# A gated state-space layer and a mixture of experts on one core: the front and first loop of the scan reordered, half a convolution given to TensorE, a new last tile, and new interleaving tables

## The chip, the cores and the metric

The kernel runs on one core of one Trainium2 chip. A core has five engines that run side by side, each with its own in-order instruction queue: TensorE (PE, matmuls; its weight loads are shown as PEld), VectorE (DVE), ScalarE (ACT), GpSimd (POOL) and SyncE (SP, which issues most DMAs). The metric is the time on the device of one execution, in microseconds (us). Three timed runs of the kernel before gave 1078.26, 1078.32 and 1080.39 us, a median of 1078.32 us. A further execution was recorded by the hardware profiler; every duration in this document that is not called a median comes from such a profiled execution.

## The reference

Four independent sequences `b`, each of L = 512 tokens. A state-space layer runs over a context and is gated by the normalised input; its result is added to the input, and a mixture of seven experts (three per token, beside one shared expert) is added to that.

```python
x   = einsum('ed,bld->bel', in_proj_w, ctx)               # 512 channels, from 256
u   = silu(causal_conv(x, conv_w, 4 taps) + conv_b)       # one filter per channel
dt, Bm, Cm = split(einsum('ke,bel->bkl', x_proj_w, u))    # 16, 16, 16 rows
delta = softplus(dt_proj_w @ dt + dt_proj_b)
for t:                                                    # scan over time, n = 16 states
    state = state * exp(delta_t * A) + (delta_t * u_t) * B_t
    y_t   = sum_n state * C_t
y = (y + D * u) * silu(layernorm(x_in))
x = x_in + tanh(g0) * y
x = x + tanh(g1) * moe(layernorm(x))                      # silu(x W1) * (x Wg) @ W2, top 3 of 7, plus shared
```

All arithmetic is fp32.

## The kernel before

**Layers and loops.** Sequence `b` is called layer `b`. Its 512 channels lie in four blocks `c` of 128 partitions, its 512 tokens in the free dimension. The scan of a layer (`loop`, from L495) goes in 32 steps; a step is one state `k` (of 16) and two channel blocks `c0`, `c0 + 1` (W = 2). For each step:

- POOL multiplies B by delta times u into `h` (`product`, L583, 1024 elements a partition);
- ACT makes the decay exp(delta A) into two PSUM banks `da` (`decay`, L594), of which there are only two in all;
- DVE runs two scans over time in `h` (L616), then multiplies `h` by C (`finish`, L541). The multiplication is called the C product here.

In layer 0 PE adds the C products of all states up in four PSUM banks `sum` by multiplying with the identity (L555), and every third C product is made by POOL rather than DVE. The C row is read from SBUF (`bc`) in the first four steps; from the fifth on ACT has copied it to a PSUM bank `c_bank` (L543) first. In layers 1 to 3 DVE makes all C products and adds them up itself (L548).

**What precedes a loop.** `in_proj` (PE, L246) fills a PSUM bank `pin`; `last_tap` (ACT, L256) and `other_taps` (DVE, L266, three instructions) are the convolution; `silu` (ACT, L272); `x_proj` (L278), `rows_out` and `load_bc` send B and C out to DRAM and back to all partitions; `dt_proj` (L298), `abs_relu`, `exp`, `log`, `rest_of_z`, `soft` make delta, `mul` (L358) the product u delta, and `d_u` (ACT, L351) the term D u. For layer 0 `front` (L425 on) does this with nothing beside it, and begins layer 1's convolution. The rest of layer 1's convolution stands in layer 0's first step (L628), all four `silu`s of layer 1 and the four gates `silus_x` are flushed after the second step (L633), and layer 1's delta is made a piece at a time during the loop (`ahead_delta`, called from `finish`, L530).

**Experts.** When a loop is done, `post` (L676) and `route` (L755) make the normalised rows and the routing, and `experts` (L990 on) the shared expert and 13 tiles of 128 routed rows, each with three weights loaded from DRAM. A tile takes 24 passes of 512 columns through PE, 8 of 128 for transposes, and a few instructions on ACT and DVE; its rows are added to the output by an indirect DMA that POOL issues (`add_rows`, L962). While the experts of sequence `q` run, the loop of layer `q + 1` and the preparation of layer `q + 2` run beside them. Their order is not left to a scheduler. `experts` is a generator with some 54 slots, and after each slot the table `STEPS[q]` says how many steps of the scan to emit and `PIECES[q]` how many pieces of the next layer's preparation. The tables thus fix in which order each in-order engine meets the work of the two. For the last sequence there is no loop left, and PE works alone.

**DMA queues.** SP issues the B and C loads (two buffers `bc`, each holding two states), the weights and the clearing of the sorted rows in DRAM (`clear`), all in program order; a load that waits for its buffer holds up what is behind it.

Where the wait lists below say `issue`, no other engine is seen to be waited for.

## Time and profile before

| what | us |
|---|---|
| median of the three timed runs | 1078.32 |
| the profiled execution | 1076.32 |
| its span, first to last instruction | 1074.5 |
| DVE busy in the span | 798.7 (74%) |
| PE busy | 948.9 (88%) |
| ACT busy / POOL busy | 544.5 / 493.7 |
| first scan of layer 0 starts | 39.80 |
| fourth C product of layer 0 done, fifth step's scans start | 69.19 |
| first transposes after loop 0 / 1 / 2 / 3 (L689) | 166.72 / 398.84 / 621.47 / 840.36 |
| mean granted TensorE clock | 0.953 |

A line of the timeline reads: start, duration, engine, source line, operation, output<-input, shape, count and, in square brackets, how long the engine had been idle before and what released it. Adjacent instructions of one kind are merged ("x4" is four of them, with one start and the busy time of all). The groups of busy time count a matmul until its modelled end, so PE at 20.00 of 20 us is not PE at its peak. Only stretches in which the engine that sets the pace is idle, or does what could be done elsewhere, can be won.

### The profile page before, as it was taken

How to read it: one execution, taken by the hardware profiler on the slowest of the kernel's cores; microseconds unless marked ns; L12 is line 12 of the kernel's file. 1: busy time of each engine (PE TensorE's matmuls, PEld its weight loads, DVE VectorE, ACT ScalarE, POOL GpSimd, SP SyncE). 2: the span in 40 equal slices, each digit the busy share in tenths (PEclk: the TensorE clock that was granted, in tenths of full speed). 3: DMA queues.
4: the chain of work that ended last, by engine and by line, in shares of the span. 5: the costliest groups of instructions: out<-in, count | busy, mean ns of one | idle time of the engine just before them, and what ended most of it. 6: DMA issues, size and time to landing. Idle time of an engine off the chain costs nothing. (4 is left out here: it accounts for less than half of the span.)

```text
span 1074.5 us, 8875 instructions
## 1 busy us (share of the span) xinstructions
PE 948.9 (88%) x2504; PEld 425.3 (40%) x2504; DVE 798.7 (74%) x992; ACT 544.5 (51%) x761; POOL 493.7 (46%) x326
## 2 busy tenths in 40 slices
PE   7377766799999987999998988889999999999995
PEld 3122223344444433444344443334444534444442
DVE  5888987999999998899999999999986521100000
ACT  5567552356687854447696755536665220122121
POOL 1278981383563653563555545755554205011111
PEclk9679888899999999999999999989999999999998
DMA  4139730198999865589899936779999459999973
GB/s 135 51 130 320 272 117 1 39 339 293 349 324 352 309 233 188 173 321 362 296 335 307 356 110 208 280 245 371 367 375 317 142 163 314 336 321 323 333 242 82
DMA packets 138044, 272.11 MB, mean 253 GB/s; under 512 B 17135, under 2 KB 17135, under 8 KB 137983
## 3 DMA queue, kind: packets, MB, share of 16 engines
q1 hardware_dynamic: 126174, 244.19, 64.4%
q0 software_dynamic: 11328, 26.42, 10.7%
q10 hardware_dynamic: 480, 0.79, 0.2%
q8 instruction: 26, 0.43, 0.2%
q14 instruction: 36, 0.29, 0.1%
HBM read 230.65 MB, written 40.71 MB: 253 GB/s over the span
## 5 line engine op out<-in xcount | busy, mean ns | idle before, releaser
L583 POOL TENSOR_TENSOR h<-bc,home 128x1024 f32<-128x1024 f32 x128 | 309.7, 2426 | 254.1 <-DVE home L548 207.7
L923 PE MATMUL p<-w,turned_x 128*128 128x512 f32 x832 | 380.0, 601 | 16.1 <-ACT turned_x L915 5.4
L616 DVE TENSOR_TENSOR_SCAN h<-da,h 128x512 f32<-128x512 f32 x256 | 297.3, 1205 | 11.9 <-POOL h L583 7.6
L594 ACT ACTIVATE da<-home,a_neg 128x512 f32<-128x512 f32 x256 | 174.7, 689 | 228.7 <-DVE h L616 224.5
L923 PEld LDWEIGHTS p<-w,turned_x 128*128 128x128 f32 x832 | 154.6, 192 | 196.8 <-issue 169.6
L923 PE MATMUL po<-w,turned_h 128*128 128x512 f32 x416 | 189.7, 599 | 6.3 <-ACT yo L957 3.6
L962 POOL DMA_INDIRECT out_dram<-yo,row x52 | 92.8, 1785 | 190.2 <-ACT yo L957 156.8
L1097 DVE TENSOR_TENSOR h<-h,p 128x512 f32<-128x512 f32 x52 | 35.1, 674 | 144.6 <-PE p L923 138.0
L541 DVE TENSOR_TENSOR h<-h,bc 128x1024 f32<-128x1024 f32 x96 | 130.9, 1363 | 1.0
L548 DVE TENSOR_TENSOR home<-home,h 128x1024 f32<-128x1024 f32 x96 | 119.5, 1245 | 3.1
L555 PE MATMUL sum<-hc,ident 128*128 128x512 f32 x128 | 75.6, 743 | 39.7 <-DVE hc L541 22.5
L923 PEld LDWEIGHTS po<-w,turned_h 128*128 128x128 f32 x416 | 75.7, 192 | 84.6 <-issue 76.0
L875 POOL DMA_INDIRECT xs<-xn,place x48 | 55.5, 1157 | 47.7 <-issue 39.4
L915 ACT COPY turned_x<-pt_x 128x512 f32<-128x512 f32 x52 | 30.2, 580 | 74.2 <-PE pt_x L910 74.2
L594 ACT ACT_TABLE_LOAD x51 | 65.4, 1283 | 0.9
L957 ACT ACTIVATE yo<-po,weight 128x512 f32<-128x512 f32 x52 | 35.6, 684 | 54.7 <-PE po L923 49.2
L555 PEld LDWEIGHTS sum<-hc,ident 128*128 128x128 f32 x128 | 28.1, 231 | 85.7 <-DVE hc L541 30.6
L923 PE MATMUL p2s<-home,w_s 128*128 128x512 f32 x128 | 61.5, 626 | 0.0
L923 PE MATMUL p1s<-home,w_s 128*128 128x512 f32 x128 | 59.5, 603 | 1.7 <-ACT sgs L1017 1.7
L1056 PE MATMUL pos<-w_s,home 128*128 128x512 f32 x128 | 57.1, 596 | 4.3 <-DVE home L1020 2.3
L915 ACT COPY turned_h<-pt_h 128x512 f32<-128x512 f32 x52 | 30.1, 578 | 48.9 <-PE pt_h L910 48.9
L1158 ACT ACT_TABLE_LOAD x36 | 46.2, 1283 | 0.5
(141 smaller groups left out, 812.7 us busy)
## 6 DMA issues: line engine op xcount, KB each, us to landing
w<-in_w_dram SPq DMA_DIRECT2D x104, 1024.0 KB, 6.6
w<-in_wg_dram SPq DMA_DIRECT2D x52, 1024.0 KB, 11.2
bc<-rows SPq DMA_DIRECT2D x32, 1024.0 KB, 7.8
xt<-xs SPq DMA_DIRECT2D x52, 256.0 KB, 4.4
xs<-empty SPq DMA_DIRECT2D x12, 780.0 KB, 16.7
w_s<-in_ws_dram SPq DMA_DIRECT2D x8, 1024.0 KB, 10.0
xx<-in_x_dram SPq DMA_DIRECT2D x4, 1024.0 KB, 7.4
w_s<-in_wsg_dram SPq DMA_DIRECT2D x4, 1024.0 KB
```

The costliest lines, as they stand in the source:

```text
L541: engine.tensor_tensor(hc, h, c_k.unsqueeze(1).to_broadcast([P, W, L]), ALU.mult)
L548: nc.vector.tensor_tensor(y[:, c0 : c0 + W, :], y[:, c0 : c0 + W, :], h, ALU.add)
L555: nc.tensor.matmul(sums[c1 + w], ident, hc1[:, w, :], start=False, stop=(k1 == NS - 1))
L583: nc.gpsimd.tensor_tensor(h, b_k.unsqueeze(1).to_broadcast([P, W, L]), layer.u[:, c0 : c0 + W, :], ALU.mult)
L594: nc.scalar.activation(da, layer.delta[:, c, :], AF.Exp, scale=a_neg[:, c, k : k + 1])
L616: nc.vector.tensor_tensor_scan(h[:, w, :], da, h[:, w, :], 0.0, ALU.mult, ALU.add)
L875: put = nc.gpsimd.indirect_dma_start(xs[q % 2], bass.IndirectOffsetOnAxis(ap=place[:, t, k : k + 1], axis=0), xns[:, t, :], None)
L915: nc.scalar.copy(t, pt)
L923: nc.tensor.matmul(p[:, 0:n], lhs(c), rhs(c), start=(c == 0), stop=(c == NC - 1))
L962: nc.gpsimd.indirect_dma_start(acc, bass.IndirectOffsetOnAxis(ap=slot_of[q][1][:, i : i + 1], axis=0), yo, None, compute_op=ALU.add,)
L1056: nc.tensor.matmul(pos[t], hTs[:, c, ts(t, P)], ws.t[2][:, c, :], start=(c == 0), stop=(c == NC - 1))
L1158: nc.scalar.activation(hs[i], p1.pop(i), AF.Silu)
```

## The change

Lines with `-` are the kernel before. The parts are:

- **Front.** Six small matmuls on the identity ahead of everything (`WARM`). `d_u` for blocks 0 and 1 of layer 0 is issued before the last `silu`, for 2 and 3 right after the logarithms. The logarithms get tiles of their own, since `y` now holds D u. The statistics of x (`norm_x`) for three blocks stand ahead of the `z` instructions, and `rest_of_z` for three blocks ahead of the first `soft`. The taps of layer 1's block 1 stand after `mul(1)`.
- **Convolution by TensorE.** For blocks 2 and 3 of layer 1 POOL builds diagonal matrices of the four taps; ACT copies `pin` to SBUF (`copy_in`), PE applies the taps by shifted matmuls (`all_taps`) in pieces of `ahead_delta`, and ACT adds the bias (`taps_out`). Eight matmul calls more on PE, beside the six of WARM, and six tap instructions fewer on DVE.
- **First loop.** All steps run over blocks first and states second; the C row goes to `c_bank` before step one, so no C product of DVE reads `bc`; the silus of layer 1 (blocks 0 and 1) and the four gates are flushed right after the first decay; those of blocks 2 and 3 come in `ahead_delta`, in a group of their own.
- **Tail.** In the last tile of the last sequence, the outputs of the tiles before it are finished first, and the second product, gate, transposes and copies go in two halves of 256 columns (`in_halves`).
- **Tables.** New `STEPS` for sequences 0, 1 and 2 and new `PIECES` for 0 and 1. Their sums are the same (34, 34 and 29 steps, 43 and 43 pieces).

```diff
 STEPS = {
-    0: ("000000", "101011010100110100110111110111110101001101101201101001"),
-    1: ("100000", "201001010010101100110201210101110110001101201101100101"),
-    2: ("000001", "111011010010110100210101101100101111002000011101000000"),
+    0: ("000000", "101011010100110100110120111101110200010101111101101001"),
+    1: ("100000", "201001001010110100110201201101110100101101201101100101"),
+    2: ("000001", "201011010000110100110200011100200110101110200111000000"),
 ...
 PIECES = {
-    0: "000000000020212021101111112021011011102021200121200201",
-    1: "000000000201110211111021211200111200221022101001202001",
+    0: "000000002010112021101100222002011020220222010002201110",
+    1: "000000101100111111111012112002022101122210211002100001",
 ...
+    spin = ps_o.tile([P, L], F32, tag="po", name="spin")
+    for _ in range(WARM):
+        nc.tensor.matmul(spin[:, 0:P], ident, ident, start=True, stop=True)
 ...
+    for c in BY_TENSOR:                       # (2, 3)
+        taps[c] = two.tile([P, DCONV, P], F32, bufs=3, name=f"taps_{c}", tag="turned")
+        nc.gpsimd.tensor_tensor(taps[c], ident..., pr[:, c, CW : CW + DCONV]..., ALU.mult)
 ...
+        def copy_in(self, c):
+            nc.scalar.copy(self.u[:, c, :], self.pin.pop(c))
+        def all_taps(self, c, ks):
+            if ks[0] == 0:
+                self.pcv = spare(f"pcv_{self.b}_{c}")
+            for k in ks:
+                nc.tensor.matmul(self.pcv[:, k:], taps[c][:, DCONV - 1 - k, :], self.u[:, c, 0 : L - k],
+                    start=(k == 0), stop=(k == DCONV - 1))
+        def taps_out(self, c):
+            nc.scalar.activation(self.u[:, c, :], self.pcv, AF.Identity, bias=pr[:, c, CB : CB + 1])
 ...
     def ahead_delta(ly):
+        for c in BY_TENSOR:
+            ly.all_taps(c, (0, 1)); yield
+            ly.all_taps(c, (2, 3)); yield
+            ly.taps_out(c); yield
+        for c in BY_TENSOR:
+            ly.silu(c)
+        yield
         ly.x_proj()
 ...
     def front():
 ...
+        for c in range(W):
+            l0.d_u(c)
         l0.silu(NC - 1)
-        for c in range(2):
-            l1.conv(c)
+        l1.conv(0)
+        l1.last_tap(1)
 ...
+        for c in range(NC - 1):
+            norm_x(0, c)
         for c in range(NC):
             l0.abs_relu(c, by_vector=True)
 ...
-            l0.log(c, own=False)
-        for c in range(W):
-            norm_x(0, c)
-            l0.w_of_z(c)
+            l0.log(c, own=("sg", "yo")[c % 2])
         for c in range(W, NC):
-            norm_x(0, c)
+            l0.d_u(c)
+        norm_x(0, NC - 1)
+        for c in range(NC - 1):
+            l0.rest_of_z(c)
         for c in range(W):
             l0.soft(c)
             l0.mul(c)
-        l1.conv(2)
+        l1.other_taps(1)
+        l1.copy_in(2)
 ...                                            # loop
-            steps[per_load:] = [(k, c0) for k in range(NG, NS) for c0 in range(0, NC, W)]
+            steps = [(k, c0) for k in range(NS) for c0 in range(0, NC, W)]
 ...
-            if sums is not None and n >= per_load:
-                if n % 3 == 2 and n < last:
+            if sums is not None:
+                if n % 3 == 2 and per_load <= n < last:
                     engine, late = nc.gpsimd, True
                 else:
                     c_k = c_bank
 ...
+            if b == 0 and n == 0:              # right after the first decay
+                szs = silus_x(b)
+                for c in range(NC):
+                    if c not in BY_TENSOR:
+                        later.append(lambda c=c: nxt.silu(c))
+                flush()
 ...
             if b == 0 and n == 0:
-                nxt.conv(NC - 1)
-                for c in range(NC):
-                    later.append(lambda c=c: nxt.silu(c))
-                szs = silus_x(b)
-            if b == 0 and n == 1:
-                flush()
+                nxt.copy_in(NC - 1)
 ...                                            # experts, the last tile of all
-            if ends:
-                second_product(i)
+            if ends:
+                out(i - 2)
+                add_rows(q, i - 3, yos.pop(i - 3))
+                add_rows(q, i - 2, yos.pop(i - 2))
+                output(i - 1, (ps_h, "p1"))
 ...
         if ends:
-            output(i - 1, (ps_h, "p1"), lambda: turn_h(i))
+            out(i - 1)
+            add_rows(q, i - 1, yos.pop(i - 1))
+            in_halves(i)
+            out(i)
```

## The prediction

> **What bounds the kernel now.** I read the busy tenths in 40 slices first, then the timeline of the first 110 us on all engines, then each stage's list of waits, and last the timelines around the longest of them.
>
> The page's busy rows (each digit is a slice of 26.9 us):
>
> ```profile
> PE   7377766799999987999998988889999999999995
> DVE  5888987999999998899999999999986521100000
> ```
>
> Three regimes. In the first 6 slices (to 160 us) no experts can run: DVE sets the pace and PE is half idle. From slice 9 to 29 both are near full. From slice 33 PE is alone. Loop 0 is a pure prologue: routing needs all of it, so what is cut there moves everything behind it.
>
> The timeline from 0 to 110 us:
>
> ```profile
> 8.26 0.78 ACT L256 ACTIVATE home<-pin,pr 128x512 f32<-128x512 f32 x1 [0.97 <-PE pin L246]
> ...
> 37.30 2.32 DVE L266 SCALAR_TENSOR_TENSOR home<-pin,pr,home 128x511 f32<-128x511 f32 x3
> 39.80 2.34 DVE L616 TENSOR_TENSOR_SCAN h<-da,h 128x512 f32<-128x512 f32 x2 [0.18 <-POOL h L583]
> 43.59 2.32 DVE L266 SCALAR_TENSOR_TENSOR home<-pin,pr,home 128x511 f32<-128x511 f32 x3 [1.46 <-ACT home L256]
> ...
> 57.19 1.28 ACT L272 ACT_TABLE_LOAD   x1
> 58.49 2.19 ACT L272 ACTIVATE home<-home 128x512 f32<-128x512 f32 x4
> 59.99 3.33 DVE L541 TENSOR_TENSOR hc<-h,bc 128x1024 f32<-128x1024 f32 x1
> 60.59 2.92 ACT L487 ACTIVATE sz<-xx,nmr,rstd_z 128x512 f32<-128x512 f32 x4
> 65.61 2.34 DVE L616 TENSOR_TENSOR_SCAN h<-da,h 128x512 f32<-128x512 f32 x2 [2.29 <-POOL h L583]
> 69.19 2.33 DVE L616 TENSOR_TENSOR_SCAN h<-da,h 128x512 f32<-128x512 f32 x2
> ```
>
> To be seen: two tap groups of layer 1 on DVE between 37 and 46 us; two DVE waits (1.46, 2.29); a C product of 3.33 us where its like takes 1.22; and ACT busy for 7.6 us with silus and table loads just when DVE needs decays.
>
> Later waits, from the timelines of their places:
>
> ```profile
> 98.76 1.22 DVE L541 TENSOR_TENSOR hc<-h,c_bank 128x1024 f32<-128x1024 f32 x1 [2.59 <-ACT c_bank L543]
> 235.06 0.75 DVE L1062 SCALAR_TENSOR_TENSOR xx<-pos,tg,xx 128x512 f32<-128x512 f32 x1 [2.04 <-PE pos L1056]
> 460.58 0.69 DVE L1020 TENSOR_TENSOR home<-sgs,p2s 128x512 f32<-128x512 f32 x1 [2.09 <-ACT sgs L1017]
> 710.41 0.69 ACT L594 ACTIVATE da<-home,a_neg 128x512 f32<-128x512 f32 x1 [0.42 <-DVE h L616]
> 711.04 0.58 ACT L915 COPY turned_x<-pt_x 128x512 f32<-128x512 f32 x1
> 711.67 6.72 PE L923 MATMUL p<-w,turned_x 128*128 128x512 f32 x8 [3.08 <-ACT turned_x L915]
> 718.66 3.60 PE L923 MATMUL p<-w,turned_x 128*128 128x512 f32 x8
> 1058.92 1.54 POOL L962 DMA_INDIRECT out_dram<-yo,row  x1 [5.76 <-ACT yo L957]
> 1064.47 1.54 POOL L962 DMA_INDIRECT out_dram<-yo,row  x1 [4.01 <-DMA out_dram<-yo,row]
> ```
>
> **The change part by part.** All against the profiled execution, 1076.32 us.
>
> *WARM.* The first input matmuls start at 4.72 when their data land, and follow each other by 0.85 us; from 8.06 on by 0.43. ACT's first tap waits 0.97 for the fourth. At 0.43 each the fourth would end near 6.6, and ACT would be held by `a_neg` (7.05 to 7.29) instead. The six calls are 12 passes of a quarter length, 2.6 us at the slow pace, from about 1.5 us (the identity is ready at 1.4), so they end before 4.72. Bounds: 0 (PE is still slow) and -0.97. I take -0.6. TensorE: Matmul & The Clock Gate (Part 1, "What's actually happening") of the Trainium skill says that PE runs at half rate until it has been busy for a window of about 3.4 us, and that the window runs freely. By that rule 2.6 us and a pause of 0.7 may or may not be enough, and this term would be 0 or -0.97.
>
> *Front to the fourth C product, on DVE.* In both kernels DVE ends layer 1's block 0 at 22.3 (WARM aside). From there the new order on DVE is: three pairs of statistics at 0.83 (to 24.8), four `z` at 0.62 (27.3), the fourth pair and `ve` (28.35), three times `w` and `rest_of_z` at 0.45 + 0.73 (31.9). The first logarithm ends at 31.4 as before (ACT's relus, table loads and exponentials end up where they were; z is only 0.3 later and the exp table load at 25.66 covers it). Then two times `soft` and `mul` at 2.17 (36.25), the taps of block 1 at 2.3 (38.6), `nmr` 0.1, `soft` and `mul` of block 2 (40.8), block 3 with its `w` and rest 3.34 as at 50.78 (44.15). Four steps of scans and C product follow at 3.6, as the steps from 69.19 on: 58.55. Before: 69.19. This term is -10.6. It consists of two tap groups of 2.3 gone, 1.46 + 2.29 of waits, 2.1 of the long C product, and 2.5 of small gaps and of work moved into the wait for the logarithm.
>
> What must cover it: the two `d_u` ahead of the last `silu` are 1.44 of ACT in an idle time of 1.59 before 18.73. The taps' diagonals are two POOL multiplications (some 1.2 each by half of L583's 2.4), after `pr` lands near 7; POOL's next need is 28. ACT after the logarithms (33.0): two `d_u` 1.44, `copy_in` 0.57, C copy 0.57 (B and C have landed by 31.2, when DMA traffic ends), table load 1.28, two decays 1.3 (38.2), table load, four gates 2.92, two silus 1.1, table load: 44.8. The next decays need a bank that the first scan frees at 45.4, so ACT is on time by 0.6, under 5.5 us of DVE work on blocks 2 and 3; that is what the 7.6 us at 57.19 lacked. In layer 1's `in_proj(3)` PE now waits for block 1's taps, since both use the bank `s`; PE's next work is at 44, it has 5 us to spare. SP's third B and C load waits for its buffer until 52 instead of 69, so the shared weights and clears behind it start earlier.
> Bounds: -8 (the gates are 2.6 late) and -12.5.
>
> SBUF — State Buffer (Terms, "shared port pair") of the Trainium skill says that DVE and GpSimd lock a port pair for a whole instruction and the loser blocks. The row agrees once (3.33 is 1.22 plus most of one 2.35 POOL product) and not always (1.22 at 56.49 with POOL busy). By the rule the new order could also lose: `soft` and `mul` of blocks 2 and 3 read two SBUF tiles, and should the first POOL product (36.3 to 38.7) slip behind the taps they would block for up to 2.3, making this term -8.3.
>
> *Rest of loop 0.* The wait of 2.59 at 98.76 comes of ACT waiting 1.80 for a `pdt` that PE holds behind sums of late POOL products, after POOL had waited 2.09 for a B load. In the new order `dt_proj` is a step ahead of its reader and the load queue starts earlier, so I count it gone: -2.6. New is the second silu group: load 1.28, two silus 1.2, load 1.28 = 3.8 on ACT between decays. It begins 3.1 after a step's first scan starts, its next decay comes at 7.6, and DVE, whose step has its C product on POOL, wants it at 5.9: +1.7. Taps on PE (16 passes, 7 us) lie in PE's idle half; the two `taps_out` at 0.7 in ACT's gaps of 1.3 to 1.8 between decays. Sum -0.9; bounds -2.6 (burst hidden) and +3.8 (burst bare, the wait replaced by another: POOL has 9.23 of work in 9.4 per three steps).
>
> *Tail.* The last add is issued at 1064.47, after waiting 4.01 for the add before it, issued at 1058.92. Tile 11's output now goes ahead of tile 12's second product: its eight passes end at 1053.9, its add follows that of tile 10 (1051.61 + 4.8) at 56.9 and lands at 61.7. Tile 12: second product to 1057.4, gate half to 57.9, transposes 58.25, copy, output 3.44 to 61.9, scale 0.7: add at 62.9. -1.5. Bounds: -1.6, and +1 if short passes cost 0.25 rather than 0.215 each and the exposed gate counts twice.
>
> *Tables.* The instruction order of the two built programs shows what moves. Sequence 0: the taps of `pin_0` now stand ahead of the `pos` addition at 235.06, and fill its 2.04; DVE paces that stage: -2.0. Sequence 1: the same taps go ahead of the product at 460.58, filling 2.09: -2.1. Sequence 2: `turned_x_0` now precedes the decays at 709.30 and 710.41 that held it; PE would start 2.5 earlier and not fall to half pace (6.72 against 3.60 for eight): up to -5.6; DVE, full until 780, must follow, and I take -3.0. Together -7.1. I can't trace all other swaps of 43 + 43 pieces. Bounds: -13 (5.6, the POOL wait of 2.63 at 455.57, and others) and +6.2 (one new stall like that at 711).
>
> Sum: -0.6 - 10.6 - 0.9 - 1.5 - 7.1 = -20.7, so 1055.6 in a profiled execution. The median of the timed runs before stands 2.0 above the profiled one; carried over: **1057.6**.
>
> **The rivals.**
> - *The tables bring nothing*: their waits are replaced by others of the same size. For it: DVE and PE are both full there, and a moved instruction delays its neighbours. Against: the three waits are visibly uncovered. 1064.7.
> - *Loop 0 gives back*: POOL, full to 98%, becomes its bound, and the silu burst is bare. +4.7 on the forecast: 1062.3, and with idle tables 1069.4. For it: B loads kept POOL waiting three times (4.8 in all). Against: the loads come earlier now.
> - *More*: sequence 2 wins its whole 5.6 and the POOL wait of 2.63 goes: 1052.4, near 1050 with the bounds of the front.
> - *Slower*: the new tables put a PE input copy behind a pair of decays, as at 711, each time 6.2 (3.1 wait, 3.1 slow PE). Without the tables' gain the forecast is 1064.7; three such places make 1083.3, and above 13.6 / 6.2 = 2.2 of them it is slower than before. For it: the orders change in hundreds of places. Against: I find the copy moved ahead where it hurt.
> - *The warm-up doesn't warm*, or the halves save nothing: +0.6 to +2.1, inside the others.
>
> **How the numbers follow.** Forecast 0.48 (its own range 1052 to 1062), idle tables 0.25, loop 0 gives back 0.12, more 0.09, slower 0.05, and 0.01 for about no change. Low 1050 takes in most of "more"; high 1069 the idle tables and most of the give-back. Within 0.2% (2.2 us) is what a measurement here can't tell from no change. Faster 0.94, same 0.01, slower 0.05.
>
> **What would show it.** Right: the scans of layer 0 start near 44 without break; the fifth step's near 57 to 58; no DVE C product over 1.3 in loop 0; the first transposes at 153 to 156; the last add waiting for ACT, not a DMA; no idle DVE at the `pos` addition and no PE wait of 3 at sequence 2's first tile. Wrong: first scans past 47 with ACT as releaser; POOL as DVE's releaser in loop 0; stages between the first transposes longer than 232, 223 and 219.

## The result and the profile after

The changed kernel took 1059.36 us, the median of four executions (1056.93 to 1061.98); the kernel before, on the same chip, 1078.29 (four, 1075.84 to 1080.39). The ratio is 0.9825 with a 95% interval of 0.9802 to 0.9848: 18.9 us faster, where 20.7 were forecast. Six later executions gave a median of 1056.11 and, against the kernel before on the same chip, a ratio of 0.9812 (0.9784 to 0.9840). The profiled execution after took 1059.25 (span 1057.2), the one before 1076.32 (1074.5): 17.1 less.

The busy rows of the page after (a digit is now 26.4 us):

```profile
PE   9587867799999897999999888899999999999995
DVE  6999978999999997899999999888999531100000
```

The shape is the old one; the prologue is half a slice shorter, and DVE is at 6 or more in each of the first 30 slices. The timeline of the front and of loop 0 shows where that half slice went:

```profile
7.29 0.76 ACT L273 ACTIVATE home<-pin,pr 128x512 f32<-128x512 f32 x1
38.92 2.93 ACT L541 ACTIVATE sz<-xx,nmr,rstd_z 128x512 f32<-128x512 f32 x4
41.75 1.13 ACT L305 ACTIVATE home<-home 128x512 f32<-128x512 f32 x2
43.48 2.33 DVE L679 TENSOR_TENSOR_SCAN h<-da,h 128x512 f32<-128x512 f32 x2
45.85 1.22 DVE L595 TENSOR_TENSOR hc<-h,c_bank 128x1024 f32<-128x1024 f32 x1
56.48 1.22 DVE L595 TENSOR_TENSOR hc<-h,c_bank 128x1024 f32<-128x1024 f32 x1
57.62 2.33 DVE L679 TENSOR_TENSOR_SCAN h<-da,h 128x512 f32<-128x512 f32 x2
84.06 2.34 DVE L679 TENSOR_TENSOR_SCAN h<-da,h 128x512 f32<-128x512 f32 x2 [1.69 <-ACT da L648]
```

ACT's first tap (L273, formerly L256) no longer waits. Gates and silus now end at 42.9, ahead of the first scans at 43.48 (L679, formerly L616), and no wait stands between these and the fifth step at 57.62, which was at 69.19. All C products (L595, formerly L541) last 1.22. The wait of 2.59 for `c_bank` is gone; the one new wait in the loop is 1.69 at 84.06, for decays that stand behind the second group of silus.

The places that the tables were to improve, on DVE, with the POOL products beside two of them:

```profile
224.22 0.75 DVE L1120 SCALAR_TENSOR_TENSOR xx<-pos,tg,xx 128x512 f32<-128x512 f32 x1 [0.65 <-PE pos L1114]
224.88 1.82 DVE L595 TENSOR_TENSOR h<-h,bc 128x1024 f32<-128x1024 f32 x1
441.31 2.95 POOL L637 TENSOR_TENSOR h<-bc,home 128x1024 f32<-128x1024 f32 x1
441.46 0.69 DVE L1078 TENSOR_TENSOR home<-sgs,p2s 128x512 f32<-128x512 f32 x1 [2.09 <-ACT sgs L1075]
442.06 3.29 DVE L595 TENSOR_TENSOR h<-h,bc 128x1024 f32<-128x1024 f32 x1
452.13 3.99 DVE L595 TENSOR_TENSOR h<-h,bc 128x1024 f32<-128x1024 f32 x1
452.67 2.36 POOL L637 TENSOR_TENSOR h<-bc,home 128x1024 f32<-128x1024 f32 x1
```

The wait at the `pos` addition fell from 2.04 to 0.65, but the C product behind it now takes 1.82 instead of 1.21. In sequence 1 DVE's 2.09 for `sgs` is still there, at another instruction, and two C products run into POOL's (L637, formerly L583) and take 3.29 and 3.99.

To see what each part brought I cut both profiles at instructions that both kernels have. Layers are counted from 0; "old" columns are of kernels with the old code or table for that stretch, "new" of kernels with the changed one, over all profiles of this study.

| stretch | profiled pair, before / after | predicted change | old, mean (profiles) | new, mean (profiles) |
|---|---|---|---|---|
| start to layer 0's fifth step | 69.19 / 57.62 | -11.2 | | |
| from there to the first gate of layer 0 | 91.69 / 91.33 | -0.9 | | |
| start to that gate | 160.88 / 148.95 | -12.1 | 162.1 (2) | 147.4 (8) |
| gate to layer 1's first scan | 25.97 / 26.17 | 0 | | |
| layer 1's first scan to layer 2's (sequence 0) | 214.54 / 214.26 | -2.0 | 214.9 (4) | 214.0 (10) |
| layer 2's to layer 3's (sequence 1) | 223.23 / 223.67 | -2.1 | 224.1 (4) | 221.8 (10) |
| layer 3's to its router passes (sequence 2) | 244.49 / 239.01 | -3.0 | 243.9 (4) | 240.1 (9) |
| router passes to the last `pos` addition | 46.02 / 46.02 | 0 | | |
| `pos` addition to the last add to the output | 149.34 / 148.88 | -1.5 | 150.2 (2) | 148.9 (9) |
| last add to the end | 10.05 / 10.22 | 0 | | |

In the profiled pair the gain of 17.3 in the span is 11.9 up to the first gate, 5.5 in sequence 2, 0.5 in the tail, and nothing in sequences 0 and 1. The last two columns say that a single pair can mislead by 2 to 3 us in a stretch.

### The profile page after: what moved, and what is told of

The parts are those of the page before. It is cut to its first block, busy times and chain, and to the rows that moved or that the text cites. A ratio compares the mean times of both kernels' runs of the same rounds, so it can differ in the third digit from the quotient of the medians.

```text
span 1057.2 us, 8951 instructions
## 1 busy us (share of the span) xinstructions
PE 952.6 (90%) x2540; PEld 430.9 (41%) x2540; DVE 798.7 (76%) x987; ACT 551.5 (52%) x770; POOL 497.4 (47%) x328
## 5 line engine op out<-in xcount | busy, mean ns | idle before, releaser
L637 POOL TENSOR_TENSOR h<-bc,home 128x1024 f32<-128x1024 f32 x128 | 309.2, 2422 | 238.6 <-DVE home L602 200.0
L981 PE MATMUL p<-w,turned_x 128*128 128x512 f32 x824 | 374.5, 598 | 12.4 <-ACT h L1238 4.7
L679 DVE TENSOR_TENSOR_SCAN h<-da,h 128x512 f32<-128x512 f32 x256 | 297.5, 1206 | 9.3 <-ACT da L648 6.8
L981 PE MATMUL po<-w,turned_h 128*128 128x512 f32 x408 | 185.4, 598 | 7.7 <-ACT yo L1015 5.1
L1020 POOL DMA_INDIRECT out_dram<-yo,row x52 | 95.9, 1845 | 189.0 <-ACT yo L1015 156.4
L595 DVE TENSOR_TENSOR h<-h,bc 128x1024 f32<-128x1024 f32 x96 | 135.8, 1415 | 1.0
L609 PE MATMUL sum<-hc,ident 128*128 128x512 f32 x128 | 69.3, 684 | 21.7 <-POOL hc L595 12.1
L973 ACT COPY turned_h<-pt_h 128x512 f32<-128x512 f32 x51 | 29.5, 578 | 44.2 <-PE pt_h L968 44.2
L609 PEld LDWEIGHTS sum<-hc,ident 128*128 128x128 f32 x128 | 25.6, 212 | 63.4 <-issue 25.7
```

What stands on the lines that cost most here:

```text
L595: engine.tensor_tensor(hc, h, c_k.unsqueeze(1).to_broadcast([P, W, L]), ALU.mult)
L609: nc.tensor.matmul(sums[c1 + w], ident, hc1[:, w, :], start=False, stop=(k1 == NS - 1))
L637: nc.gpsimd.tensor_tensor(h, b_k.unsqueeze(1).to_broadcast([P, W, L]), layer.u[:, c0 : c0 + W, :], ALU.mult)
L679: nc.vector.tensor_tensor_scan(h[:, w, :], da, h[:, w, :], 0.0, ALU.mult, ALU.add)
L973: nc.scalar.copy(t, pt)
L981: nc.tensor.matmul(p[:, 0:n], lhs(c), rhs(c), start=(c == 0), stop=(c == NC - 1))
```

## The experiments

Each is the changed kernel with one thing altered, if not said otherwise. Executions of one program lie up to 8 us apart (10 for the kernel before), so differences under some 2 us are read from the profiles' stretches and not from the times.

**1. The old tables for sequences 0 and 1.**

```diff
-    0: ("000000", "101011010100110100110120111101110200010101111101101001"),
-    1: ("100000", "201001001010110100110201201101110100101101201101100101"),
+    0: ("000000", "101011010100110100110111110111110101001101101201101001"),
+    1: ("100000", "201001010010101100110201210101110110001101201101100101"),
 ... and PIECES 0 and 1 likewise
```

> The changed kernel with the old tables for sequences 0 and 1; sequence 2 keeps its new one. Theory (after the result): in those two sequences the filled waits came back as longer DVE products, so undoing them costs nothing: time 1059 within 1.5; first scans of layers 1, 2, 3 lie 214.5 and 223.2 apart, as before the change (changed kernel: 214.3 and 223.7); the 2.04 and 2.09 and 2.63 waits of DVE are back, and the 32 C products of each of these loops shrink from 44.1 and 44.4 to 42.3 and 42.5. Rival (the prediction's terms): slower by 4.1, 1063. Rival 2: the new front made the stages slower by itself and the tables hid that: slower by more than 5.

Measured: 1057.62 (1056.64 to 1060.42), no slower. The stretches were 215.29 and 225.07, that is 1.0 to 1.8 and 1.2 to 4.0 above the profiles with the new tables. DVE's waits were back: 2.03 in layer 1's stretch, 2.63 and 2.09 in layer 2's. (A further 4.75 there, before a scan, has its like in the changed kernel: 4.64.) The C products of layer 2's loop took 42.5 together instead of 44.4, and those of layer 1's 43.5 instead of 44.1. So what the new tables save in waits (1.4 and 2.6) returns in good part as longer products. In layer 2 it is always the same two: the sixth takes 3.27 to 3.29 in all ten profiles with the new table, 1.22 in the four with the old one; the seventh 3.97 to 4.00 against 2.86 to 2.88. Of the 4.1 forecast for both sequences the times show nothing.

**2. The old table for sequence 2 alone.** The `STEPS` string of sequence 2 put back.

> The changed kernel with the old table for sequence 2 alone. Theory: the whole wait at this sequence's first tile returns, with the half-speed passes behind it, and nothing in the sequences after it takes it up: slower by 5.0 to 5.6, 1064.6; TensorE waits about 3.1 at the first tile's first product and its eight passes take 6.7 instead of 3.6. Rival (the prediction's term): DVE's fullness gives part of it back, slower by 3.0. Rival 2: the 5.5 come of other swaps in this table or of the front, and the wait does not come back or costs under 1.

Measured: 1060.32 (1058.51 to 1061.46), 2.0 to 2.7 over the two kernels timed beside it that keep the new table (experiments 1 and 4). The stretch took 244.51, as before the change. But the wait that I had made responsible was not what came back. TensorE at the first tile's first product, in this kernel and in a second profile of the unaltered kernel before:

```profile
694.63 3.70 PE L981 MATMUL p<-w,turned_x 128*128 128x512 f32 x8 [1.54 <-ACT turned_x L973]
```

```profile
713.09 3.70 PE L923 MATMUL p<-w,turned_x 128*128 128x512 f32 x8 [1.48 <-ACT turned_x L915]
```

The eight passes take 3.70 after 1.5 of waiting, where the first profile had 6.72 after 3.08. The stall of 6.2 that the forecast leaned on is there in two of the four profiles with the old table (the first one, and experiment 9); in the other two it is a wait of 1.5. And the stretch does not follow it: 244.49 and 242.95 with the long stall, 243.82 and 244.51 without.

**3. The same, with one loop step moved behind the copy of the first tile's input.**

```diff
-    2: ("000001", "201011010000110100110200011100200110101110200111000000"),
+    2: ("000001", "111011010000120100210101101100101111002000011101000000"),
```

(The old string has `1110110100101101...`; its eleventh digit, the step, is moved on by three.)

> The changed kernel with the old table for sequence 2, of which one digit is moved: the one loop step whose decays stood ahead of the first tile's input copy is now issued behind that copy. Theory: this one step makes the wait, so this kernel has most of the new table's gain: 1 to 1.5 above the changed kernel's 1059.3, and some 4 under the kernel with the whole old table; TensorE waits under 1 at the first tile and its passes take 3.7. Rival: the gain is spread over the 20 or so other moved steps; then this kernel gains under 1.5 against the whole old table. Rival 2: the wait moves on to the next copy, which now has two steps' decays ahead of it, and nothing is gained.

Measured: 1061.41 (1060.02 to 1061.80), and 245.88 for the stretch: nothing is gained against the old table, 1.4 lost. The second rival holds, as TensorE and ACT show:

```profile
693.75 3.70 PE L981 MATMUL p<-w,turned_x 128*128 128x512 f32 x8 [0.67 <-ACT turned_x L973]
706.63 5.46 PE L981 MATMUL p<-w,turned_x 128*128 128x512 f32 x8 [5.31 <-ACT h L1238]
```

```profile
697.58 0.69 ACT L648 ACTIVATE da<-home,a_neg 128x512 f32<-128x512 f32 x1 [3.88 <-DVE h L679]
698.69 0.69 ACT L648 ACTIVATE da<-home,a_neg 128x512 f32<-128x512 f32 x1 [0.42 <-DVE h L679]
702.35 0.69 ACT L648 ACTIVATE da<-home,a_neg 128x512 f32<-128x512 f32 x1 [2.97 <-DVE h L679]
703.46 0.69 ACT L648 ACTIVATE da<-home,a_neg 128x512 f32<-128x512 f32 x1 [0.42 <-DVE h L679]
704.09 0.58 ACT L973 COPY turned_x<-pt_x 128x512 f32<-128x512 f32 x1
704.68 1.28 ACT L1238 ACT_TABLE_LOAD   x1
705.98 0.60 ACT L1238 ACTIVATE h<-p 128x512 f32<-128x512 f32 x1
```

The first tile's copy is early, its wait is 0.67, as in the changed kernel. The second tile's copy and the silu now stand behind four decays, which wait for DVE's scans, and TensorE waits 5.31. A step moved in one place has to be paid for in the next; the new table pays for it over the whole sequence. Summed over the stretch, TensorE's idle times of more than 0.3 come to 16.6 to 18.3 us with the old table (four profiles) and to 13.6 to 15.2 with the new one (nine): less at the first tile (0.7 against 1.5 to 3.1), and no gap of 1.2 some 186 us in; the rest is spread.

**4. Without the spinning matmuls.** The six matmuls at L151 are left out.

> The changed kernel without its six spinning matmuls. Theory: the first input products again run at half pace, the fourth ends about 1 later, ACT's first tap starts at 8.2 instead of 7.29, and all that is behind it shifts by 0.97: first scan of layer 0 at 44.4 instead of 43.48; time 1.0 longer. Rival 1 (the prediction's value): 0.6. Rival 2: the front is bound by DVE's own work, and the delay is swallowed before the first scan: 0.

Measured: 1058.31 (1056.73 to 1060.74), no difference that can be measured. ACT's first tap starts at 8.50, the first scan on DVE at 43.91:

```profile
8.50 0.78 ACT L269 ACTIVATE home<-pin,pr 128x512 f32<-128x512 f32 x1 [1.28 <-PE pin L259]
```

In this pair of profiles the spins win 1.2 at the first tap. Over all profiles it is less: the tap starts at 7.29 to 8.01 in the eleven with the spins and at 8.26 to 8.50 in the three without. The input passes fall from 0.85 to 0.43 apart from the third to the fifth pass on with the spins, from the fifth or sixth without. At the first scan 0.25 to 0.6 are left (43.32 to 43.67 with the spins). The rest is swallowed on the way: with spins DVE waits 0.31 and 0.50 for ACT's exponentials and logarithms, without them not at all.

**5. All taps of layer 1 on DVE, all four silus before the first decay.**

```diff
-BY_TENSOR = (2, 3)
+BY_TENSOR = ()
-        l1.copy_in(2)
+        l1.conv(2)
+        l1.conv(3)
 ...
-            if b == 0 and n == 0:
-                nxt.copy_in(NC - 1)
```

> The changed kernel with all four blocks of layer 1's convolution on DVE, all of them ahead of the first scan, and so all four silus in one group before the first decay. Theory: two tap groups of 2.3 are back on DVE's path and the second silu group in loop 0 is gone with its wait of 1.69: first scan at 48.1 instead of 43.48, no wait of DVE at 84, end of loop 0 later by 4.6 - 1.7 = 2.9; time 1062.2. Rival 1: the two groups fit into DVE's waits and cost under 1, while the burst is saved: faster by about 1. Rival 2: ACT's group of four silus comes too late for the decays as it did before the change: first scans broken by a wait of 2 or more, slower by 5 or more.

Measured: 1061.85 (1060.99 to 1065.46), 4.3 above experiment 7a, which was timed beside it and whose front is the changed one. The first scans start at 50.23, 6.7 later, of which 2.20 are a wait that my arrangement made (`pin_3` shares its bank with block 1's taps, and so its copy comes late):

```profile
42.50 2.31 DVE L283 SCALAR_TENSOR_TENSOR home<-pin,pr,home 128x511 f32<-128x511 f32 x3 [2.20 <-ACT home L273]
50.23 2.33 DVE L680 TENSOR_TENSOR_SCAN h<-da,h 128x512 f32<-128x512 f32 x2
```

In the loop the wait of 1.69 is gone, and DVE waits nowhere longer than 0.2 between the first scan and the first gate. So the two prices are as the sum had them: 2.3 for each tap group, 1.7 for the second group of silus.

**6. The C product of the first four steps from SBUF.**

```diff
-                else:
+                elif n >= per_load:
                     c_k = c_bank
 ... and no copy to c_bank before the fourth step
```

> The changed kernel with the C product of the first four steps read from the loaded rows in SBUF, not from the copy in PSUM; two copies by ACT go. Theory (one of four collides with a POOL product, as before the change): one product of 3.3 instead of 1.22, fifth step 2.1 later, time 1061.4. Rival 1: all that run beside a POOL product are held: 4 to 8 later, 1063 to 1067. Rival 2: the long product of the kernel before had another cause than the row's place, and all four stay at 1.22: no change, 1059.3.

Measured: 1058.67 (1057.78 to 1061.60); the first gate comes at 151.52, 4.1 later than the mean of the changed front. The times show little of it, but the profile shows it whole. First POOL's run of five products, with the second of them by itself, then DVE's C products, and last a POOL product of the kernel before:

```profile
43.48 13.52 POOL L637 TENSOR_TENSOR h<-bc,home 128x1024 f32<-128x1024 f32 x5 [5.59 <-DVE home L395]
45.78 3.34 POOL L637 TENSOR_TENSOR h<-bc,home 128x1024 f32<-128x1024 f32 x1
```

```profile
45.68 1.23 DVE L595 TENSOR_TENSOR hc<-h,bc 128x1024 f32<-128x1024 f32 x1
49.19 3.31 DVE L595 TENSOR_TENSOR hc<-h,bc 128x1024 f32<-128x1024 f32 x1
54.78 3.31 DVE L595 TENSOR_TENSOR hc<-h,bc 128x1024 f32<-128x1024 f32 x1
60.43 1.23 DVE L595 TENSOR_TENSOR hc<-h,bc 128x1024 f32<-128x1024 f32 x1
```

```profile
56.58 3.34 POOL L583 TENSOR_TENSOR h<-bc,home 128x1024 f32<-128x1024 f32 x1
```

POOL's five products run back to back from 43.48 to 57.0. Of the three C products in that time two, which begin 0.11 after a POOL product of 2.34, are held for 2.08 each. The first begins 0.09 ahead of POOL's second product and is not held, but that POOL product takes 3.34 instead of 2.34. So each time one of the two is held, the one that begins later. The same is seen in the kernel before: its C product at 56.49 takes 1.22, and the POOL product that begins at 56.58 takes 3.34. With the row in PSUM all four C products take 1.22, and POOL's 2.34 to 2.36. The Trainium skill ("SBUF — State Buffer", Terms, "shared port pair") has DVE and GpSimd arbitrate for a port pair that is locked for a whole instruction; these durations agree with that. On DVE's path the copy to PSUM from the first step on is worth two such blocks here, one more than the profile before had shown; which engine is held hangs on 0.1 us.

**7. The last tile: whole (a), and in halves with two banks (b).**

```diff
 (a)        -            in_halves(i)
 (a)        +            second_product(i); gated(i); turn_h(i); copy_h(i); output(i)
 (b)        -            p2i = ps_h.tile([P, D], F32, tag="p2", ...)
 (b)        +            p2s = [ps_h.tile(... tag="p2" ...), ps_a.tile([P, L], F32, tag="da", ...)]
 (b)        and p2s[k] for p2i in the product and the gate of half k
```

> The changed kernel with the last tile's second product, gate and transposes whole instead of in halves; tile 11's output still goes ahead of them. Theory: the halves themselves bring little, since in the changed kernel TensorE's second half waits 0.58 for the first half's gate: from the start of tile 12's first product to the last add 21.2 instead of 20.86, time 0.3 longer. Rival 1 (the prediction, which had the halves hide half of gate and copy): 0.9 longer. Rival 2: the halves cost more than they hide, and the whole one is 0.3 faster.

> The changed kernel with the two halves of the last second product in two PSUM banks instead of one. Theory: the wait of 0.58 is DVE's gate on the bank that TensorE wants to go on writing; with a bank of its own the second half does not wait: no wait of TensorE between the halves, last add 0.5 earlier after the start of tile 12's first product (20.4 instead of 20.86). Rival 1: the gate of the first half then runs beside the second half and the wait moves to the second gate's end: gain 0.1 or less. Rival 2: the add before the last holds the last one (4.8 between them) and takes half of it.

Measured: 1057.59 (1054.36 to 1058.45) and 1055.76 (1052.90 to 1058.54). The stretch from the last `pos` addition to the last add was 149.33 and 148.34, and 148.87 to 148.88 in nine profiles of kernels with the changed tail, so there it can be read to 0.1. It varies where the last add waits for the one before it: 149.34 and 151.05 in the two profiles of the kernel before, and 149.19 in the kernel with spins of experiment 8, which has two banks like (b). The changed tail, then (a) and (b), and then the last add in the second profile of the kernel before and in the kernel of experiment 8:

```profile
1036.83 1.89 PE L1176 MATMUL p<-w,turned_x 128*128 128x256 f32 x8
1039.30 1.99 PE L1176 MATMUL p<-w,turned_x 128*128 128x256 f32 x8 [0.58 <-DVE h L1179]
1041.13 0.38 PE L1182 MATMUL pt_h<-ident,h 128*128 128x128 f32 x2
1046.95 1.54 POOL L1020 DMA_INDIRECT out_dram<-yo,row  x1 [4.49 <-ACTq L1029]
```

```profile
1036.38 0.66 PE L968 MATMUL pt_h<-ident,h 128*128 128x128 f32 x4 [0.85 <-DVEq L1029]
1037.77 3.70 PE L981 MATMUL po<-w,turned_h 128*128 128x512 f32 x8 [0.73 <-ACT turned_h L973]
```

```profile
1031.24 1.89 PE L1179 MATMUL p<-w,turned_x 128*128 128x256 f32 x8
1032.96 1.89 PE L1179 MATMUL p2b<-w,turned_x 128*128 128x256 f32 x8
1034.69 0.38 PE L1185 MATMUL pt_h<-ident,h 128*128 128x128 f32 x2
```

```profile
1066.95 1.54 POOL L962 DMA_INDIRECT out_dram<-yo,row  x1 [5.72 <-DMA out_dram<-yo,row]
1047.08 1.54 POOL L1029 DMA_INDIRECT out_dram<-yo,row  x1 [4.81 <-DMA out_dram<-yo,row]
```

Putting tile 11's output first gains nothing by itself against the first profile of the kernel before (149.33 for 149.34) and 1.7 against the second: what it takes off the DMA is paid as a bare gate and a bare copy (0.85 and 0.73). The halves gain 0.46 of that. With a second bank the second half need not wait for DVE to have read the first: from the first half to the transposes behind the second it is 3.45 (1031.24 to 1034.69) instead of 4.30 (1036.83 to 1041.13). Of these 0.85 the last add had 0.54 in the profile of (b), and nothing in the other profile with two banks, where it waited for the add before it; there the second rival holds. That the second bank shortens the whole is thus not shown. The sixteen half passes follow each other by 0.216, as the forecast had them; the 1.89 of a line reaches to the modelled end of its last pass, which overlaps what comes next.

**8. The spread: the changed kernel and the one before again, and spins in three more waits of TensorE.** The last has two banks as in 7b, 10 and 6 spinning matmuls ahead of the last sums of loop 0, 16 and 10 ahead of the transposes of the normed rows in sequences 0 and 1.

> The changed kernel once more, unaltered, for the spread between executions of one program. Theory (after the first runs): two places of this program cost 2 to 3 more in some executions than in others, because TensorE comes out of a wait of 3 at half pace: the eight sum passes at the end of loop 0 (3.7 or 6.6) and the eight router passes of sequence 1 (3.6 or 5.5). So this profile has the one or the other value at each of the two, and its stages between are the same as in the first one within 0.5: loop 0 from first scan to first gate 103 or 105.5, layer 2 from scan to scan 221.2 or 223.7; time between 1053.5 and 1062. Rival: the spread lies elsewhere, evenly over the stages.

> The kernel before once more, for the same reason. Theory: same stages as in its first profile where TensorE's pace does not enter (layer 1 scan to scan 214.5, from sequence 2's first scan to the last router passes 244.5, from pos addition to last add 149.34), and loop 0 and layer 2 at 121.1 and 223.2, or up to 2.5 less where the passes there run at full pace. Rival: the stage of sequence 2 varies by several us too, and its gain of 4.6 in the changed kernel is luck.

> The changed kernel with the last tile's two halves in two banks, and with spinning matmuls on TensorE in three of its waits: 10 in the wait of 3 before the last sums but one of loop 0, 6 before the last ones, 16 and 10 ahead of the transposes of the normed rows of sequences 0 and 1. Theory: TensorE comes out of these waits at full pace in every execution, the sums take 3.7 and the router passes of sequence 1 3.6, and the slower half of the executions goes: median 1053, all within 2. Against the changed kernel on the same chip 4 to 6 faster. Rival 1: the spins are themselves late or slow and push the work behind them: no gain, or a loss of 1 to 2. Rival 2: the spread has another cause, and median and spread stay where the kernel with two banks had them, 1055.8 and 5.6.

Measured: 1056.11 (1054.07 to 1060.75) for the changed kernel, 1078.67 for the one before (one execution), 1058.37 (1054.71 to 1063.09) with the spins. In the profile of the changed kernel the sums at the end of loop 0 were slow again and the router passes of sequence 1 fast; that execution's layer 2 took 221.12, with 2.13 of waiting where the first had 4.64. These stretches are as the theory had them. First the slow values (first profile of the changed kernel), then the second profile of the same program, then experiment 2, which is the same code up to sequence 2:

```profile
143.43 6.61 PE L609 MATMUL sum<-hc,ident 128*128 128x512 f32 x8 [3.04 <-POOL hc L595]
411.62 5.54 PE L820 MATMUL pl<-home,gw 128*7 128x512 f32 x8 [1.61 <-ACT home L767]
```

```profile
143.40 6.64 PE L609 MATMUL sum<-hc,ident 128*128 128x512 f32 x8 [3.03 <-POOL hc L595]
410.78 3.60 PE L820 MATMUL pl<-home,gw 128*7 128x512 f32 x8 [2.17 <-ACT home L767]
```

```profile
143.52 3.70 PE L609 MATMUL sum<-hc,ident 128*128 128x512 f32 x8 [0.90 <-POOL hc L595]
```

So part of the spread lies in these places: eight passes take 3.6 to 3.7 or up to 6.6 after a wait, and what waits for them is 2 to 3 later. The granted clock of the same traces goes with it. The next lines read: window, its length, PE's busy time, then the clock as a share of full speed, the DMA's busy share and GB/s. They are the sums and the router passes of the first profile, the router passes of the second, and the sums of experiment 2:

```profile
143.43:149.30 5.87, 5.87 (x7) 0.50 0.51 179
411.62:415.50 3.88, 3.88 (x5) 0.50 0.39 128
```

```profile
410.78:414.38 3.60, 3.60 (x9) 1.00 0.39 146
```

```profile
143.52:147.22 3.70, 3.70 (x8) 1.00 0.70 234
```

In all fourteen traces this clock keeps one value for 3.41 us or a whole multiple of it, and the steps lie differently against the program in each execution: counted from the first instruction, 2.54 past a multiple of 3.41 in the first profile of the changed kernel, 0.25 in experiment 2. So the same wait can leave the next passes at half clock in one execution and at full clock in another. What sets where the steps lie is not shown.

The second profile of the kernel before has 243.82 for the stretch of sequence 2 (244.49 in the first), so the rival, that this stage varies by several us, is not borne out. But its loop 0 took 123.2 from first scan to first gate instead of the 121.1 expected at most, with one wait for `c_bank` of 5.24 where the first profile had 2.59, and its tail the 151.05 of experiment 7.

With the spins both places were fast in the profile (3.60 and 3.60), but the slow passes turned up elsewhere:

```profile
638.98 5.03 PE L829 MATMUL pl<-home,gw 128*7 128x512 f32 x8 [2.82 <-PEq L1038]
850.27 5.20 PE L829 MATMUL pl<-home,gw 128*7 128x512 f32 x8 [2.71 <-PEq L1038]
```

The router passes of sequences 2 and 3 were slow, the stretch from the latter to the last `pos` addition took 47.62 instead of 46.02, and the median was 2.3 above the changed kernel's on the same chip, with intervals that overlap. My theory that the spins would take away the slower executions fell. Whether spinning in more places would cure it was not tried.

**9. All old tables, front, loop 0 and tail as changed.** Experiments 1 and 2 together.

> The changed kernel with all the old tables, sequences 0, 1 and 2; front, loop 0 and tail as changed. Theory (stages of the runs so far): sequence 0 costs 0.3 to 1.0, sequence 1 1.3, sequence 2 4.6, together 6.2 to 6.9 above the changed kernel's 1057.8 (mean of its ten runs): 1064 to 1064.7; first scan of layer 3 to its router passes 244, against 238.8 to 239.0. The prediction's value: 7.1. Rival: what the runs with single old tables gave by their times alone, none for sequences 0 and 1 and 2 for sequence 2: 1060.

Measured: 1061.22 (1059.78 to 1064.48, six executions), ratio to the kernel before 0.9836 (0.9808 to 0.9864); the stretches 214.43, 225.01 and 242.95. Against the mean of the changed kernel's ten executions, 1057.8, the mean of these six is 3.7 longer; by the ratios to the kernel before (0.9825 and 0.9812 with the new tables) the difference is 1.2 to 2.6. Neither 6.2 nor the 7.1 of the prediction; nearer to the rival's 1060. The three stretches of the table above differ by 0.9 + 2.3 + 3.8 = 7.0 in the mean, more than the times bear out; part of that is that the router passes of sequence 1 were slow in all four profiles with an old table for sequence 1 (5.30) and in two of the ten with the new one. By chance alone so uneven a split would come in some 1 of 67 cases, so it may belong to the old table; no run was made to tell.

## Why the prediction was right, and where not

The time, 1059.36, lies 1.8 above the forecast and inside the range, and most of the gain came from where it was put. By its own steps, against the profiled pair:

- *Front to the fourth C product, -10.6, with WARM -11.2*: measured -11.6 (69.19 to 57.62). Predicted start of the scans 44.15, less 0.6; measured 43.48. ACT's chain of gates and silus was to end at 44.8 and ended with its table load at 44.2. What each piece is worth was shown apart: 2.3 a tap group (5), two blocked products of 2.08 (6), where the sum had one of 2.1. The forecast's list of what the term consists of does not add up: with two tap groups it makes 12.95, and without its 2.5 of small gaps 10.45; the -10.6 itself came from the order on DVE. And the row at 56.49, which the forecast read as speaking against a block, shows one: POOL's product beside it was the one held, 3.34 for 2.34 (6).
- *WARM, -0.6*: the first tap moved by the full 0.97 in the pair, and by 0.25 to 1.2 over all profiles, but only some 0.25 to 0.6 reached the first scan (4). The mean was near in part by luck: I had left open how warm TensorE gets, and what swallowed the rest was ACT's chain behind it.
- *Rest of loop 0, -0.9*: the wait of 2.59 went, the burst of silus came at 1.69. Over the whole stretch -0.4 in the pair, since the last sums ran at half pace and the first gate waited 2.53 (1.90 before). In five of the eight profiles they ran fast and the first gate came 1.9 to 2.6 earlier than in the pair. No term of the sum had this.
- *Tail, -1.5*: measured -0.46 in the pair, -2.2 against the second profile of the kernel before. The step that failed is the end of the second product: I had eight whole passes' time, 3.5, from 1053.9 to 1057.4; it took 4.30, because the second half waits for DVE's gate on the first one's bank. The short passes themselves cost what was counted (3.45 with two banks). The last add did wait for ACT and not for a DMA, as said. But the 4.8 that the sum had from one add to the next was too short: where the last add waits for the one before, they lie 5.55, 6.35 and 7.26 apart, and this makes the old tail vary.
- *Tables, -7.1*: this is the term that was most off. By the times of experiment 9 they bring 1.2 to 3.7. The step "the taps fill the 2.04 and the 2.09" saw the first wait go (2.04 to 0.65); the 2.09 stayed, and the 2.63 for POOL went in its place. It counted a filled wait as a gain. Over half came back where DVE, no longer waiting, met POOL's product in the same memory: 1.82 for 1.21, 3.29 for 1.22, 3.99 for 2.87. The step for sequence 2 named the wrong cause: the stall at 711 was 6.2 long in two profiles and 1.5 of waiting in two others, with no effect on the stretch (2), and moving the step that made it only moved it (3). The stretch did get shorter, by 5.5 in the pair and 3.8 in the mean, because several waits of TensorE each became a little smaller (3), which the forecast had only in its lower bound, as "others".
- *Of the rivals* "the tables bring nothing", 1064.7, overstates as much as the forecast did: the kernel with old tables took 1061.2. "Loop 0 gives back" did not occur: POOL released no wait of DVE in loop 0. "Slower" neither: TensorE waits 0.67 at sequence 2's first tile.
- *What would show it*: the first transposes came at 154.79 (153 to 156 was said). Between them lay 234.9, 220.2 and 214.0; the first is longer than the 232 that was to speak against the change (232.1 before). TensorE has the same 560 matmuls between the two transposes in both kernels; in this profile eight of them took 6.66 after a wait of 2.87, and in the second profile of the changed kernel the stage is 233.1. By DVE's last gates it is 231.6, as before (231.7).

So the sum was right to 2 us partly by luck, with two errors that cancel in part: the tables gave 3 to 6 less than booked, and front and loop 0 gave more. By the times, the kernel with old tables is 18.7 us under the kernel before on the same chip (medians 1061.22 and 1079.90), where the terms without tables add up to 13.6; the means over the profiles give 14.7 up to the first gate and 1.3 in the tail. What makes up the rest is not settled; there are only two profiles of the kernel before.

The kernel with two banks for the last tile (7b) is the fastest that was run: 1055.76, ratio 0.9792 (0.9721 to 0.9863) to the kernel before. That it gains on the changed kernel (0.54 in one profile's tail, a loss of 0.31 in the other's) is not shown.

## What to carry to other kernels

A prologue that nothing overlaps is the place where terms add up as in a sum: what was taken off DVE's path there came out to within 0.4 us, and each part could be priced from rows of the profile. Where several engines are full, a filled wait is only a gain if the filler does not then meet another engine's work in the same memory, and a stall seen in one profile is worth a second profile before it is booked. Compare stretches between the same two instructions over several profiles; where TensorE leaves a wait of 2 to 3 us, expect its next passes at full or at half pace, or some of each, and read the granted clock beside them.

## What the runs showed of the hardware

- After a wait of some 1.5 to 3 us TensorE's next eight passes of 512 columns took 3.6 to 3.7 in some executions and up to 6.7 in others of the same code, with a granted clock of 1.00 and 0.50. The clock changed only at steps 3.41 us apart, which lay differently in each execution. Over the fourteen traces, every such stretch at full clock behind which the clock stayed full had TensorE busy for 0.41 of it or more, and every one at half clock behind which it rose for 0.80 or more. The Trainium skill ("TensorE: Matmul & The Clock Gate", Part 1, "What's actually happening") says that the pace is set by activity in a window that runs freely, not from the kernel's start, and that the same kernel therefore counts different numbers of slow passes in different executions. That agrees with the profiles above. Spins of 2.4 us (20 quarter passes) ahead of the sums went with 3.60 behind them, in the one profile there is.
- After 2.9 us of spins and a pause of 0.4 or less, the input passes ran at full pace (0.43 apart) from the third to the fifth on, in eleven profiles; without spins from the fifth or sixth, in three.
- Of three C products on DVE that read and write SBUF beside POOL's, two took 3.31 and one 1.23, and beside that one POOL's product took 3.34 instead of 2.34: the one that began later, by 0.1 us, was held. With one operand in PSUM neither was (four of four took 1.22).
- With both halves of a product in one PSUM bank, TensorE waited 0.58 with the second until DVE had read the first, and the whole took 4.30; with two banks it took 3.45 and waited nothing. Whether the chip asks for this wait or only the program's own guard of the bank is not shown.
